# Mirrored score blocks through HBM in pieces of 512 bytes, with columns in runs of 32, and a new plan order

## The chip, the cores and the metric

The kernel runs on one core of a Trainium2 chip. The metric is the device time of one execution in microseconds (us); the time given is the median of several runs.

## The reference

Sixteen graphs (batches) of 1024 nodes with 128 features pass through four layers, all in float32, each with a residual: `x = x + layer(relu(layernorm(x)), adj)`. `adj` is a dense 1024 x 1024 matrix per batch, of which about 1.6% is non-zero.

```python
# layer 0, three times (i = 0, 1, 2; relu on all but the last)
h = h @ W[i] + b[i]
nh = h / norm(h)
h = (adj * (nh @ nh.T)) @ h
# layer 1
h = relu(((1 + eps) * h + adj.T @ h) @ W1 + b1) @ W2 + b2
# layer 2: attention, tanh(s1[i] + s2[j]) where adj > 0, softmax over j, times h
# layer 3: e = (h @ A) @ h.T; e = e + e.T; softmax(where(adj > 0, e, 0), axis=1) * adj, times h,
#          then three sigmoid gates per node
```

Two score matrices are symmetric: `nh @ nh.T` in layer 0 and `e + e.T` in layer 3. A batch that uses both has four such products of 1024 x 1024: three in layer 0 and one in layer 3.

## The kernel before

**Tiling.** Nodes are cut into 8 blocks of 128. A score matrix is made row block by row block (j = 0 to 7), each in two halves of four column blocks (`HALVES`, s = 0 and 1), and each half is one PSUM tile of 128 x 512 called `sq`. From it the VectorEngine (DVE) makes the weights: `ew = sq * rn * adjT` at line 1589 in layer 0, or the masked scores `e` with their maximum at line 1854 in layer 3. The TensorEngine (PE) then accumulates the weights with `h` into PSUM tiles `acc` (line 1422 by rows of 512, line 1433 by nodes of 128).

**The symmetric half.** `Square.row` computes only blocks on and above the diagonal (line 1360). A block below it is the transpose of one above. `Square.keep` saves those above from PSUM into the tile `above`, 22 blocks of 128 columns, at the places that `PLACE` gives. There are two ways back:

- Near the diagonal, the ScalarEngine (ACT) copies the blocks (line 1392), and PE transposes them when the lower row comes (line 1370).
- For the quarter of rows 4 to 7 by columns 0 to 3, in products where `by_dma` holds (batches 1 to 13, 13 x 4 = 52 products), DVE transposes every 32 x 32 square within the 128 x 512 tile (line 1382, four times in a product). After rows 1 and 3, `send` puts eight blocks into a buffer in HBM (`by_hbm`, line 1402, one DMA of 512 KB), and four DMAs of 128 KB bring the squares back to their mirrored places in the tile `got` (line 1413). `row` then hands out `got` in place of a PSUM tile for rows 4 to 7, s = 0.

In `by_hbm`, a row of 128 floats holds four squares that belong to four different partition groups of `got`, so a read moves pieces of 32 floats, 128 bytes.

**Other DMAs.** The transposed adjacency (`adjT`, line 1509) and some transposes of node features (`squares`, line 1186) use the same way of 32 x 32 squares, with pieces of 128 bytes. `adjL` (line 1467) and `x` (line 1450) come in longer pieces. All of them and the mirrored blocks are issued on the SyncEngine's queue (SP).

**Order.** The program is not written in its order of execution. Each operation is recorded with an engine, an estimated time, what it reads and writes, and a due time from the table `TIMES` (plus `PERIOD` per batch; the suffixes `<0`, `<1`, `>1`, `>0` are for the first two and last two batches, the key without a suffix for those between). `Plan.order` walks through estimated time: it takes the engine that can start earliest, and among that engine's operations ready within `WINDOW` (0.05 us) of it the one with the lowest rank:

```python
due = TIMES[o.key + o.edge if o.key + o.edge in TIMES else o.key][o.nth]
o.rank = (o.batch * PERIOD + due, o.seq)
```

`POOLS` and `KINDS` set how many buffers of a kind there are, how many may be held at once, and how many by batches younger than the oldest. So several batches run through one another, and every engine carries out its instructions in the order of the plan. The plan charges 0.35 x 2 us for a `by_hbm` write and 1.8 x 2 us for the four `got` reads, with latencies of 2.2 and 2.4 us.

**Names for the steps.** `psP` is the projection of `hT` with a weight (line 1200); `hT` is evicted from `acc` by ACT (line 1222); `hTn` is the transpose of `h`, the operand of the square; `rn` holds the inverse squared norms.

Of the kernel before, what the change touches and what calls it, by code (L numbers as in the profile page):

```python
# [12 lines left out]
ALU = mybir.AluOpType  # L13
AX = mybir.AxisListType

P = 128
# [205 lines left out]
def tile_adj_preln(  # L222
# [102 lines left out]
    for load_it in first:  # L325
# [13 lines left out]
        "adjT": ("adjT", 16, 16), "adjL": ("adjL", 5, 5), "x": ("x", 3, 3), "w4": ("big", 11, 5),  # L339
        "chunk": ("big", 13, 11), "above": ("above", 2, 2), "got": ("got", 1, 1), "ps": ("bank", 8, 7),  # L340
        "acc": ("bank", 8, 7), "small": ("small", 7, 18), "row": ("row", 5, 6), "hbm": ("hbm", 3, 3),
# [5 lines left out]
        "T DMA raw <0": [49.7, -29.05, 16.55, 2.15, 37.95, 6.2, 10.3, 13.25],  # L347
        "T PE raw <0": [7.8, -3.3, -0.1, -1.05, 0.65, 10.35, 23.15, 14.4, 9.05, 23.7, 22, 29.65, 26.65, 30.6,
            38.9, 41],
        "T ACT adjT <0": [2.9, 32.7, 7.85, 8.05, 13.45, 9.6, 13.2, 15.2, 18.4, 28.65, 29.8, 34.35, 33.9,  # L350
            38.45, 39.6, 39.65],
        "T DVE su <0": [54],
        "x DMA x <0": [49.15, -28],
        "0 DVE st <0": [5.7, 4.2],
        "0 DVE mv <0": [9.65],
        "0 POOL rstd <0": [2.6],
        "0 DVE nb <0": [9.1],
        "0 DVE hn <0": [9.1],
        "0 ACT hn <0": [30.5],
        "0 PE ps <0": [-0.85, -4.05],  # L360
        "0 ACT hT <0": [-21.45, 7.65],
        "00 PE psP <0": [6.6, -12.45],
        "00 DVE h <0": [14.75, 13.15],
        "00 PE ps <0": [21.35, 2.95],
        "00 ACT hTn <0": [11.15, 11.6],
        "00 ACT sq <0": [5.15, 12.1],
        "00 DVE ss <0": [2.95, 17.5, 18.2],
        "00 POOL rn <0": [30.3],
        "00 PE sq <0": [4.2, 22.45, 6.05, 6.9, 12, 7.4, 9.35, -26.35, 5.2, 26.95, 20.6, 21.8, 29.65, 25.9,
            26.55, 27.25, 31.3, 42.4, 46.3, 24.05, 51.65, 46.5],  # L370
        "00 ACT above <0": [12.45, 21.55, 15.8, 17.1, 16.7, 22.75, 22.65, 30.8, 38.15, 35.2],
        "00 DVE ew <0": [20.65, 22.5, 22.6, 36.95, 26.95, 33.7, 29.1, 35.05, 29.6, 44.15, 35.25, 41.45, 48.8,
            51.7, 45.3, 54.4],
        "00 PE acc0 <0": [0, 11.1, 10.4, 9.05, 15.65, 16.65, 19.7, 23.2, 28.65, 45.65, 34.25, 39.85, 31.35,
            54.3, 44.2, 64.05],
        "00 POOL params <0": [35.05, 40.7, 43.85, 51.55, 56.35, 57.25, 76.7],
        "00 DMA params <0": [52.85],
        "00 DVE params <0": [65.65, 68.1, 68.15, 77.5, 77.95],
        "00 PE params <0": [50.55, 59.35, 66.9],
        "00 ACT hT <0": [51.3, 54],  # L380
        "01 PE psP <0": [47.6, 63.65],
        "01 DVE h <0": [69.95, 78.75],
        "01 PE ps <0": [61.05, 52.95],
        "01 ACT hTn <0": [69.25, 72.45],
        "01 ACT sq <0": [69.7, 71.15],
        "01 DVE ss <0": [76.45, 78.15, 75.45],
        "01 POOL rn <0": [84.25],
        "01 PE sq <0": [68.25, 64.9, 66.25, 69.95, 68.2, 60.6, 70.8, 71.45, 81.95, 78.25, 78.75, 81.15,
            80.55, 85.85, 84.35, 87.05, 85.5, 86.8, 87.75, 84.5, 87.75, 79.1],
        "01 ACT above <0": [72.2, 74.55, 76.2, 75.5, 83.2, 81.35, 84.35, 84.75, 92.9, 94.75],  # L390
        "01 DVE ew <0": [78.15, 92.4, 81.55, 86.8, 87.85, 85.5, 93, 91.7, 93.05, 101.05, 89.5, 98.7, 96.5,
            111.15, 94.25, 91.55],
        "01 PE acc0 <0": [72.7, 84, 78.85, 78.6, 79.65, 78.25, 84.45, 78.05, 85.7, 85.9, 84.65, 87.6, 87.45,
            91.5, 89.15, 92.05],
        "01 ACT hT <0": [97, 99.95],
        "02 PE psP <0": [92.4, 92.15],
        "02 DVE h <0": [111.65, 105.7],
        "02 PE ps <0": [94.65, 94.55],
        "02 ACT hTn <0": [109.1, 104.6],
        "02 ACT sq <0": [106.2, 98.2],  # L400
        "02 DVE ss <0": [108.35, 109.3, 110.85],
        "02 POOL rn <0": [131.5],
        "02 PE sq <0": [103.1, 100.15, 107.65, 110, 101.65, 105.05, 100.95, 91.9, 107.7, 108.8, 108.7, 114,
            114.45, 111, 117.45, 118.85, 121.8, 110.4, 111.4, 123.9, 120.8, 128.25],
        "02 ACT above <0": [109.85, 113, 103.2, 116.3, 113.65, 115.55, 120.5, 124.45, 131.85, 139.8],
        "02 DVE ew <0": [113.25, 106.15, 118, 112.45, 125.7, 120.05, 121.65, 124.9, 130.25, 128.35, 126.65,
            132.8, 124.95, 126.9, 123, 141.6],
        "02 PE acc0 <0": [90.15, 114.45, 106.85, 103.9, 110.45, 112.95, 116.3, 111.45, 125.35, 117.1, 121.95,
            130.1, 112.45, 124.05, 123.15, 120.6],
        "02 DVE x <0": [136.55, 141.55],  # L410
        "T DMA adjT <1": [-129, -138.55, -158.15, -107.7, -154.45, -138.3, -107.8, -104.7],
        "T DVE adjT <1": [-118.3, -111.9, -110.5, -104.85, -101.8, -89, -85.8, -85.05],
        "T ACT adjT <1": [-117.75, -118.25, -112.75, -111.85, -103.3, -98.6, -96, -94.9],
        "1 DVE st <0": [135.95, 138.05],
        "1 DVE mv <0": [141.5],
        "1 POOL rstd <0": [134.7],
        "1 DVE nb <0": [144.5],
        "1 DVE hn <0": [140.8],
        "1 ACT hn <0": [134.3, 134.75],
        "1 DVE x <0": [146.55, 166.45, 168],  # L420
        "1 DMA adjL <0": [49.7, 59.55, 62.4, 63.35, 48, 159, 152, 151.35],
        "1 DVE adjL <0": [80.85, 77.2, 82.45, 79, 78.25, 151.75, 156.5, 161.35],
        "1 PE acc1 <0": [134.5, 135.3, 136.2, 137, 138.5, 133.15, 142.35, 139.75, 142.8, 141.1, 147.5,
            146.05, 148.15, 145.4, 151.95, 150.35],
        "1 ACT g <0": [157.9, 152.5],
        "1 PE py <0": [148.1, 149.8, 154.65, 147.75],
        "1 ACT y1 <0": [150.4, 163, 157.05, 152.1],
        "1 PE py2 <0": [152.35, 154.2],
        "2 DVE st <0": [171.4, 171.55],
        "2 DVE mv <0": [176.05],  # L430
        "2 POOL rstd <0": [176.55],
        "2 DVE nb <0": [173.9],
        "2 DVE hn <0": [173.85],
        "2 ACT hn <0": [184, 172.8],
        "2 PE ps <0": [162, 177.1],
        "2 ACT hnT <0": [180.45, 171.9],
        "2 DVE alone <0": [56.3],
        "2 DVE x <0": [183.6, 216.45, 216.65],
        "2 PE psP <0": [180.2, 166.35, 167.75],
        "2 ACT h <0": [176.5, 180.2, 180.6],  # L440
        "2 DVE hrow <0": [176.1],
        "2 PE pf <0": [171.3],
        "2 ACT hfl <0": [183.15],
        "2 PE pt <0": [174.35],
        "2 ACT sr <0": [180.15],
        "2 DMA sd <0": [283.8],
        "2 DMA s1 <0": [230.2],
        "2 DVE h <0": [175.5],
        "2 ACT e2 <0": [186.9, 189.9, 184.6, 189.95, 190.8, 191.25, 189.25, 193.65, 194, 192.5, 194.7, 197.1,
            198.05, 200.15, 199.1, 197.05],  # L450
        "2 DVE e2 <0": [195.1, 187.55, 193.65, 194.5, 199.55, 199.6, 196.4, 198.2, 201.75, 200.6, 203.8,
            206.9, 206.25, 208.1, 207.45, 208.75],
        "2 PE acc2 <0": [186.85, 186.2, 184.15, 189.1, 194.4, 197.45, 194.9, 188.8, 187.75, 198.65, 189.3,
            188.2, 194.8, 201.05, 196.95, 200.75, 197.1, 199.85, 195.55, 197.6, 198.5, 195, 197.75, 199],
        "2 DVE rden <0": [210.05, 211, 214.85, 213.35],
        "3 DVE st <0": [214.65, 213.1],
        "3 DVE mv <0": [246.2],
        "3 POOL rstd <0": [230.15],
        "3 DVE nb <0": [191.15],
        "3 DVE hn <0": [197.2],  # L460
        "3 ACT hn <0": [220.35, 225.45],
        "3 PE ps <0": [220.35, 209.3, 217.3, 213.95],
        "3 ACT hnT <0": [217.95, 221.55],
        "3 PE pg <0": [214.85, 222.65],
        "3 ACT gT <0": [221.05, 225.75],
        "3 PE psP <0": [228.55, 206.05, 224.15],
        "3 DVE h <0": [228.15, 223.85, 227.05],
        "3 ACT h3T <0": [219.7, 220],
        "3 ACT mask <0": [8.25, 18.4, 14.05, 26, 16.05, 23.05, 27.85, 30.25, 28.2, 40.5, 248.85, 250, 222.55,
            229.15, 237.05, 239.9],  # L470
# [679 lines left out]
    def by_block(t, w=D, n=NB):  # L1150
        return t[:, 0 : n * w].rearrange("p (c d) -> p c d", d=w)
# [976 lines left out]
```

## Time and profile before

| | us |
|---|---|
| median of 3 runs (2389.21 to 2389.68) | 2389.58 |
| the profiled execution | 2389.48 |
| its span, first to last instruction | 2387.7 |
| PE busy | 2349.2 |
| DVE busy | 2029.0 |
| ACT busy | 1435.5 |

The span is what the profile divides up; 1.8 us of the profiled execution lie around it. A busy time is the union of an engine's instructions. A matmul's end is modelled in the profile and overlaps the next one's start, so a PE that counts as busy may still have lost time between two starts. In rows of groups, "x" is a count, then come busy us and the mean ns of one, then the idle time just before and what ended it. The DMA share is the mean over the core's 16 DMA engines; it can exceed 1 where packets overlap.

### The profile page before, as it was taken

Reading aid. Unit: us, or ns where it says so; the run is one execution under the profiler, and the core shown is the slowest. Engines: PE = TensorE matmul, PEld = TensorE weight load, DVE = VectorE, ACT = ScalarE, POOL = GpSimd, SP = SyncE. Lnnn points to the kernel's source line nnn. Section 1 sums busy time; section 2 is a strip of 40 time slices with the busy share of each in tenths; the row PEclk is TensorE's granted clock in tenths of the full one; section 3 lists DMA queues with packets and bytes.
Section 4 is the critical chain, followed back from the end, with each engine's and each line's share of the span. In section 5 each row is a group of like instructions: output and inputs, shape, how many; then the busy total and the mean of one; then the engine's idle time right before and its main releaser. Section 6 shows DMA issues by size and latency. Waiting matters only on the chain.

```text
span 2387.7 us, 35098 instructions
## 1 busy us (share of the span) xinstructions
PE 2349.2 (98%) x11577; PEld 1548.5 (65%) x11577; DVE 2029.0 (85%) x5570; ACT 1435.5 (60%) x2561; POOL 246.8 (10%) x168
## 2 busy tenths in 40 slices
PE   8999999999999999999999999999999999999997
PEld 5568566675766657666575666757576575765764
DVE  6658798898988989899898988989899888987676
ACT  7325765756566465755756657465765656655475
POOL 3001010100101101010100101001011010110012
PEclk9999999999999999999999999999999999999999
DMA  9342949879596886959779497796968869165000
GB/s 197 85 107 63 172 91 180 153 128 178 115 177 141 139 171 130 171 123 166 157 129 181 108 181 146 137 164 130 171 139 149 164 129 169 45 107 124 1 27 18
DMA packets 1316743, 314.31 MB, mean 132 GB/s; under 512 B 1108441, under 2 KB 1298017, under 8 KB 1316561
## 3 DMA queue, kind: packets, MB, share of 16 engines
q1 hardware_dynamic: 1296400, 301.35, 67.6%
q10 hardware_dynamic: 19264, 9.70, 1.4%
q8 instruction: 92, 1.51, 0.3%
q0 software_dynamic: 896, 1.01, 0.2%
q14 instruction: 91, 0.74, 0.1%
HBM read 227.50 MB, written 84.47 MB: 131 GB/s over the span
## 4 chain that ended last, share of the span: by engine, by line
PE 85%; DMA 5%; SPq 4%; ACT 3%; DVE 3%; issue 1%; DVEq 0%; ACTq 0%
PE acc L1422 33%; PE sq L1360 18%; PE acc L1433 17%; PE psP L1200 6%; PE sq L1370 4%; DMA by_hbm<-above 2%; PE py L1210 2%; DMA got<-by_hbm 2%; PE py L1651 2%; SPq L1413 1%; SPq L1509 1%; PE ps_hTn L1169 1%; PE pg L1210 1%; DVE ew L1589 1%; DMA adjT<-in_adj_dram 1%
## 5 line engine op out<-in xcount | busy, mean ns | idle before, releaser
L1422 PE MATMUL acc<-ew,h 128*128 128x512 f32 x1024 | 486.4, 597 | 8.0 <-DVE ew L1589 8.0
L1589 DVE SCALAR_TENSOR_TENSOR ew<-sq,rn,adjT 128x512 f32<-128x512 f32 x612 | 436.4, 740 | 59.4 <-PE sq L1370 24.4
L1360 PE MATMUL sq<-hTn 128*128 128x512 f32 (+3 forms) x1152 | 439.4, 488 | 0.8 <-ACT hTn L1222 0.4
L1392 ACT COPY above<-sq 128x384 f32<-128x384 f32 (+3 forms) x432 | 167.6, 393 | 365.1 <-PE sq L1370 263.1
L1360 PEld LDWEIGHTS sq<-hTn 128*128 128x128 f32 x1152 | 196.3, 191 | 148.0 <-issue 99.8
L1422 PEld LDWEIGHTS acc<-ew,h 128*128 128x128 f32 x1024 | 180.2, 191 | 169.9 <-issue 132.4
L1433 PEld LDWEIGHTS acc<-h,ew 128*128 128x128 f32 x2048 | 245.4, 192 | 35.9 <-issue 21.7
L1433 PE MATMUL acc<-h,ew 128*128 128x128 f32 x2048 | 253.3, 275 | 3.2 <-DVE ew L1589 3.2
L1433 PEld LDWEIGHTS acc<-h,e 128*128 128x128 f32 x2048 | 235.0, 192 | 17.2 <-issue 12.8
L1422 PE MATMUL acc<-e,hs 128*128 128x512 f32 x512 | 241.1, 594 | 1.3 <-ACT hs L1904 0.8
L1433 PE MATMUL acc<-h,e 128*128 128x129 f32 x2048 | 236.6, 275 | 1.1 <-DVE e L1763 1.1
L1422 PE MATMUL acc<-adjL,hn 128*128 128x512 f32 x512 | 232.9, 592 | 0.0
L1162 POOL TENSOR_TENSOR rstd<-ve,mhalf 128x8 f32<-128x8 f32 x64 | 105.0, 1641 | 1166.5 <-DVE ve L1281 1166.5
L1370 PEld LDWEIGHTS sq<-ident,above 128*128 128x128 f32 x960 | 124.4, 141 | 100.2 <-issue 76.5
L1854 DVE CUSTOM_DVE_ANT_0 e<-mask,sq 128x512 f32<-128x512 int8 x204 | 137.4, 680 | 60.6 <-ACT above L1392 53.2
L1520 ACT ACTIVATE adjT<-adjT 128x1024 f32<-128x1024 f32 x120 | 126.6, 1055 | 97.8 <-DVE adjT L1517 90.4
L1895 DVE TENSOR_TENSOR e<-e,adjT 128x512 f32<-128x512 f32 x248 | 166.1, 680 | 18.2 <-ACT e L1886 18.1
L1382 DVE STREAM_TRANSPOSE above<-sq 128x512 f32<-128x512 f32 x208 | 145.7, 706 | 35.5 <-PE sq L1360 35.5
L1370 PE MATMUL sq<-ident,above 128*128 128x128 f32 x960 | 172.5, 273 | 1.5 <-ACT above L1392 1.5
L1763 DVE SCALAR_TENSOR_TENSOR e<-adjT,e 128x512 f32<-128x512 f32 x256 | 162.3, 689 | 5.5 <-ACT e L1759 5.3
L1422 PEld LDWEIGHTS acc<-adjL,hn 128*128 128x128 f32 x512 | 93.6, 190 | 102.3 <-issue 90.9
L1517 DVE STREAM_TRANSPOSE adjT<-adjT 128x1024 f32<-128x1024 f32 x120 | 148.6, 1239 | 8.8 <-DMA adjT<-in_adj_dram 8.4
(164 smaller groups left out, 3587.2 us busy)
## 6 DMA issues: line engine op xcount, KB each, us to landing
adjL<-in_adj_dram SPq DMA_DIRECT2D x128, 512.0 KB
adjT<-in_adj_dram SPq DMA_DIRECT2D x480, 128.0 KB
by_hbm<-above SPq DMA_DIRECT2D x104, 512.0 KB
got<-by_hbm SPq DMA_DIRECT2D x416, 128.0 KB
s<-sd SPq DMA_DIRECT2D x15, 512.0 KB
out_dram<-z ACTq DMA_DIRECT2D x15, 512.0 KB
d_hT<-hn SPq DMA_DIRECT2D x14, 512.0 KB
hT<-d_hT SPq DMA_DIRECT2D x56, 128.0 KB
```

Source lines behind the costliest of these rows:

```text
L1200: nc.tensor.matmul(dst.t[:, (c - lo) * n : (c - lo + 1) * n], cols(srcT.t, c), w, start=True, stop=True)
L1360: lambda: nc.tensor.matmul(dst.t[:, (first - lo) * P :], cols(leftT.t, j), span(rightT.t, first, hi), start=True, stop=True),
L1370: nc.tensor.transpose(cols(dst.t, r), cols(above.t, p), ident)
L1382: lambda: nc.vector.transpose(span(above.t, p, p + 4), read.t),
L1392: lambda: nc.scalar.copy(span(above.t, p, p + hi - first), read.t[:, (first - lo) * P :]),
L1422: lambda s=s, lo=lo, hi=hi: nc.tensor.matmul(acc[s].t, cols(h.t, at, w), span(ew.t, lo, hi), start=(j == 0), stop=(j == NB - 1)),
L1433: nc.tensor.matmul(a.t[:, (c - lo) * n : (c - lo + 1) * n], cols(ew.t, c), h.t[:, at * w : at * w + n], start=(j == 0 and c == lo), stop=( ...
L1517: dve(V(N), [t], [t], lambda t=t: nc.vector.transpose(t.t, t.t), True)
L1589: lambda view=view, ew=ew, rn=rn, j=j, lo=lo, hi=hi: nc.vector.scalar_tensor_tensor(by_block(span(ew.t, lo, hi), D, 4), view(), rn.t[:, j ...
L1763: lambda e=e, j=j, lo=lo, hi=hi: nc.vector.scalar_tensor_tensor(span(e.t, lo, hi), span(aT[j].t, lo, hi), 0.0, span(e.t, lo, hi), op0=ALU. ...
L1854: lambda e=e, view=view, mask=mask, peak=peak, s=s, lo=lo, hi=hi: nc.vector.tensor_tensor_reduce(by_block(span(e.t, lo, hi), D, 4), by_blo ...
L1895: lambda e=e, j=j, lo=lo, hi=hi: nc.vector.tensor_mul(span(e.t, lo, hi), span(e.t, lo, hi), span(aT[j].t, lo, hi)),
```

## The change

Three things change.

1. `keep`: DVE's transpose of a 32 x 32 square stays, but it reads its PSUM tile and writes `above` in another order. The eight blocks of a pair of rows are laid out as (h, r, q, i): h is the place of a square within its 128 columns (four of them), r the row of the pair, q the column block (four), i the 32 columns of a square. One block of 128 floats now holds four squares that go to the same partition group of `got`.
2. `send` and `row`: the write to HBM keeps its pieces of 512 bytes. Each of the four reads takes 256 whole rows of 128 floats, in pieces of 512 bytes, into 32 partitions of `got`. In `got`, the 512 columns of a row q are then no longer four runs of 128 but 16 runs of 32, each 128 floats from the next, and the DVE operations that read it (lines 1589 and 1854) get views of 16 x 32 for all their operands; with a PSUM tile their views stay 4 x 128.
3. `TIMES`: nearly all due times are replaced, and the limits in `KINDS` for `w4`, `chunk`, `above`, `ps`, `acc`, `small` and `row` change. `POOLS`, `PERIOD`, `AHEAD`, `WINDOW` and the costs that the plan charges for the DMAs are the same.

```diff
-        "adjT": ("adjT", 16, 16), "adjL": ("adjL", 5, 5), "x": ("x", 3, 3), "w4": ("big", 11, 5),
-        "chunk": ("big", 13, 11), "above": ("above", 2, 2), "got": ("got", 1, 1), "ps": ("bank", 8, 7),
-        "acc": ("bank", 8, 7), "small": ("small", 7, 18), "row": ("row", 5, 6), "hbm": ("hbm", 3, 3),
+        "adjT": ("adjT", 16, 16), "adjL": ("adjL", 5, 5), "x": ("x", 3, 3), "w4": ("big", 9, 5),
+        "chunk": ("big", 10, 12), "above": ("above", 2, 1), "got": ("got", 1, 1), "ps": ("bank", 7, 8),
+        "acc": ("bank", 7, 8), "small": ("small", 7, 16), "row": ("row", 3, 3), "hbm": ("hbm", 3, 3),
...
-        "00 DVE ew <1": [-96, -97.05, -94.35, -97.1, -95.9, -87.65, -86.4, -88, -83.3, -75.3, -82.2, -75.35,
+        "00 DVE ew <1": [-97.85, -102.05, -94.45, -97.2, -96, -87.75, -86.5, -88.1, -93.95, -75.4, -82.3, -74.75,
...
-        "00 PE acc0 <1": [-98.65, -96.15, -97.8, -100.25, -96.3, -85.8, -86.2, -91.2, -92.3, -98.5, -80.2,
+        "00 PE acc0 <1": [-97.5, -95, -96.65, -85.6, -83.9, -76.4, -85, -84, -103.3, -86.3, -79.05, -75.15,
...
-        "01 ACT hT": [59.4, -161.95],
-        "02 PE psP": [11.7, 50.15],
+        "01 ACT hT": [71.05, 59.7],
+        "02 PE psP": [46.1, 46.55],
...
+    def like(v, t):
+        return t.rearrange("p (x i) -> p x i", i=v.shape[2])
...
-                return self.got, lambda: self.got.t.rearrange("p (r c d) -> p c r d", r=QUARTER, d=P)[:, q]
+                return self.got, lambda: self.got.t.rearrange("p (x q i) -> p q x i", q=QUARTER, i=SQ)[:, q]
...
-                    lambda: nc.vector.transpose(span(above.t, p, p + 4), read.t),
+                    lambda: nc.vector.transpose(
+                        self.apart(j // 2).rearrange("p (h r q i) -> p r h q i", r=2, q=QUARTER, i=SQ)[:, j % 2],
+                        read.t.rearrange("p (q h i) -> p h q i", h=P // SQ, i=SQ),
+                    ),
...
+        def apart(self, pair):
+            return span(self.above.t, 6 + 8 * pair, 14 + 8 * pair)
...
             def squares_to_places():
-                src = by_hbm.t.rearrange("(x j) (g i) -> g j x i", j=SQ, i=SQ)
-                for g in range(P // SQ):
-                    dst = span(got.t, lo * 4, hi * 4)[g * SQ : (g + 1) * SQ]
-                    with nc.allow_non_contiguous_dma(reason="squares"):
-                        nc.sync.dma_start(dst.rearrange("p (x i) -> p x i", i=SQ), src[g])
+                src = by_hbm.t.rearrange("(h y j) f -> h j y f", h=P // SQ, j=SQ)
+                dst = by_block(span(got.t, lo * 4, hi * 4))
+                for h in range(P // SQ):
+                    nc.sync.dma_start(dst[h * SQ : (h + 1) * SQ], src[h])
...
-                            by_block(span(ew.t, lo, hi), D, 4), view(), rn.t[:, j : j + 1],
-                            by_block(span(aT[j].t, lo, hi), D, 4), op0=ALU.mult, op1=ALU.mult,
+                            like(view(), span(ew.t, lo, hi)), view(), rn.t[:, j : j + 1],
+                            like(view(), span(aT[j].t, lo, hi)), op0=ALU.mult, op1=ALU.mult,
```

The `TIMES` entries shown are those that the prediction speaks of; the reads of `e` from `got` at line 1854 change as those of `ew` do.

## The prediction

> **What bounds the kernel now.** I read the engine totals first, then the chain, then PE's own waits, and only then the DMA side.
>
> ```profile
> PE 2349.2 (98%) x11577; PEld 1548.5 (65%) x11577; DVE 2029.0 (85%) x5570; ACT 1435.5 (60%) x2561; POOL 246.8 (10%) x168
> ...
> PE 85%; DMA 5%; SPq 4%; ACT 3%; DVE 3%; issue 1%; DVEq 0%; ACTq 0%
> ```
>
> PE is busy 98% of the span and is 85% of the chain that ended last. Because ends of matmuls are modelled, I also took the start-to-start times of the matmuls in the trace, by width. The lower quartile is 429 ns for 512 columns and 109 to 111 ns for 128 to 131. At those pitches all 11,577 matmuls take 2311.8 us. The rest of the 2387.7 us span is 7.3 us before the first matmul, 10.8 us after the start of the last, and 57.8 us of lost time between; 44.4 us of that sits in 186 gaps over 30 ns, and 12.9 us of those 44.4 in the first 100 us. The change adds and removes no PE instruction, so **the 44 us are all that it can win or multiply**. The waits of PE and DVE say whose they are:
>
> ```profile
> PE acc L1422 <- DVE ew L1589: 8.0, 8, 4.3
> ...
> PE psP L1200 <- ACT hT L1222: 3.2, 13, 0.3
> ```
>
> ```profile
> DVE ew L1589 <- DMA got<-by_hbm: 22.7, 18, 8.2
> ```
>
> Columns: total us, times, longest us. The largest wait of PE is for `ew`, and more than half of it is one wait of 4.3 us. DVE in turn has one wait of 8.2 us for `got`, the tile that the change touches. The timeline puts both in one place, in batch 1's first product:
>
> ```profile
> 58.20 7.13 SPq L1413 DMA_DIRECT2D got<-by_hbm  x8
> ...
> 69.48 2.74 DVE L1589 SCALAR_TENSOR_TENSOR ew<-got,rn,adjT 128x512 f32<-128x512 f32 x4 [8.23 <-DMA got<-by_hbm]
> 70.28 2.07 PE L1422 MATMUL acc<-ew,h 128*128 128x512 f32 x2 [4.25 <-DVE ew L1589]
> ```
>
> ```profile
> 60.00:66.00 6.00, 6.00 (x15) 2.42 (x13) 0.89 (x2) 2.12 (x4) 0.00 (x0) 1.00 1.33 179
> 66.00:72.00 6.00, 1.75 (x3) 0.83 (x3) 2.52 (x4) 0.37 (x1) 0.00 (x0) 0.78 1.14 300
> 72.00:78.00 6.00, 6.00 (x13) 3.04 (x12) 2.42 (x5) 0.66 (x2) 0.00 (x0) 0.65 0.20 81
> ```
>
> In the windows the last three numbers are PE clock, DMA share and GB/s. The DMA engines are overfull (1.33, 1.14) while the eight `got` reads go through; PE then waits, and comes back at a clock of 0.65.
>
> [...] the 4.25 us wait is followed by a clock of 0.65. [...] on q1 the packet records average 15.6 ns for 128 B and 28.6 ns for 512 B, so four times the bytes take 1.83 times as long. [...] No row of this trace has runs of 32 words with hops.
>
> **The change, part by part.**
>
> (1) Reads of `got`. 416 DMAs of 128 KB stay 416, but each goes from 1024 pieces of 128 B to 256 of 512 B. Before: 416 x 1024 x 15.6 ns / 16 engines = 415 us of DMA time in the span. After: 416 x 256 x 28.6 / 16 = 190 us. So q1's 67.6% should fall by 225 / 2388 = 9.4 points, to some 58%. For one read of four DMAs: 4.0 us becomes 1.8 us. At 58.20 us there are eight: 8.0 becomes 3.7, which is 4.3 us earlier. `ew` would start near 65.2 instead of 69.48, and end at 65.9. PE ran out of other work at 66.03 (the last transpose starts at 65.70 and takes 0.33), so **the wait of 4.25 us goes**. With it goes the slow clock: 0.35 x 6 us in 72 to 78, and half of the 1.7 us run after 70.28, together 3.0 us. Sum 7.3 us.
>
> In the middle I find three more `got` waits that PE feels, at 1168, 1312 and 1889 us: DVE waits 0.93, 1.24 and 1.36, all shorter than the 2.2 us that a read saves, and PE waits 0.2, 0.5 and 0.6, sum 1.3 us. What is late next there is the product itself: at 815 and 1104 us the same instruction waits 1.75 us for PE's `sq`, and no DMA helps that. The other `got` waits are under PE work and are worth nothing. The writes `by_hbm` keep 1024 pieces of 512 B: nothing.
>
> (2) The same transposes with pieces, and reads in runs of 32. The rows now:
>
> ```profile
> L1382 DVE STREAM_TRANSPOSE above<-sq 128x512 f32<-128x512 f32 x208 | 145.7, 706 | 35.5 <-PE sq L1360 35.5
> ...
> L1589 DVE SCALAR_TENSOR_TENSOR ew<-got,rn,adjT 128x512 f32<-128x512 f32 x156 | 112.0, 748 | 37.2 <-DMA got<-by_hbm 22.7 <-PE sq L1360 5.9 <-PE acc L1433 5.5
> ```
>
> The second line is matched by 740 ns for the form from PSUM, so where the operand lies hardly matters. I take 706 and 748 for after as well[...]. Below: the shortest transpose seen is 673 ns, 33 x 208 = 7 us of DVE time, all under PE. [...] The cover is DVE's idle time, 359 us in all, but only 6 to 14 us per 100 us in the middle[...]. I take nothing.
>
> (3) Order and limits. Nearly every due time moves, and so do the limits on buffers held at once (`w4` 11 to 9, `row` 5,6 to 3,3, and so on). No instruction is added. In the first two batches the PE numbers mostly rise by 1.1, those of ACT by 5.35 and those of DVE fall by 0.1; since an engine's instructions are ranked against one another only, that keeps most of the start's order. In the interior it doesn't: the 126 ACT numbers move by 8 on average, with a spread of 24. The trace of before can't price this. Below: the 13 waits for `hT` cost PE 0.41 us each as a gap (5.4 us), an early gap at 39.6 us costs 1.5, and half the 7.7 us of gaps in the last 88 us could go: 11 us. Above: the third rival. I take zero.
>
> Sum against the profiled execution (2389.48 us, 1.8 us of it outside the span, 0.1 under the median): 2389.5 - 7.3 - 1.3 = 2380.9. The median stands so close that I forecast **2381 us**.
>
> **Rivals.**
> *The wait stays in another form.* The new numbers rank batch 1's first `ew` from `got` some 10.6 earlier (-83.3 to -93.95) and its accumulation 11 earlier (-92.3 to -103.3), and the same DMA queue gets adjacency loads in another order. DVE is served in order, so if this instruction stands further forward, the 4.3 us that the read gains are given back: other `ew` behind it wait[...]. Then only the 1.3 us of the middle is won: 2388. For it: the two full windows hold 1.33 x 6 + 1.14 x 6 = 14.8 us of DMA work, and `got` is at most 8.0 of it. Against it: the plan still charges a read 3.6 us, so it does not place the consumer earlier than the data by its own reckoning.
>
> *Slower: the eviction of `hT` loses its place.* In the interior, the second half of `hT` after the second product (L1222) was due at -161.95, ahead of everything that ACT had ready; now it is due at 59.7, behind whatever is ready with a lower number. Behind it PE has only four transposes and then the projection `psP`, in order. ACT is 60% busy, and its common instructions take 1.05 us (`adjT`, `mask`) to 1.14 us (`e`). One of these in front in each of 13 batches costs 13 x 1.14 = 14.8 us if PE has nothing else placed there: 2381 + 15 = 2396. It decides from 8.6 / 13 = 0.66 us lost per batch, one such instruction in 8 of 13 batches. For it: PE already waits there 13 times. Against it: the projection's own numbers move too (11.7 and 50.15 to 46.1 and 46.55), so other PE work may be put in front.
>
> **How the numbers follow.** The forecast gets 0.60; its own range is 2369 (with the 11 us) to 2385. The wait that stays gets 0.16, at 2385 to 2393. The slower case gets 0.24, of which 0.04 is for transposes or reads that double; 2394 to 2405. A measurement of this kernel can tell 0.2% (4.8 us) from no change. So: faster 0.60, same 0.16, slower 0.24. The range 2366 to 2398 leaves out about a tenth at each end.
>
> **What would show it.** Right: q1 falls to about 58% and its packets by 416 x 768 = 319,488 to some 977,000; no wait for `got` above 4 us near 70 us, and no clock under 0.9 in that stretch; `above` transposes near 706 ns and `ew` from `got` near 748. Wrong in (1): packets fall and the clock still dips there. Wrong in (2): a transpose above 1.0 us, and DVE above 90% busy. Wrong in (3): more than 5 us of new PE waits for `hT`, `ew` or `e` in the middle. PE busy should fall by a few us, its instructions stay 11,577.

## The result, and the profile after

| | before | after |
|---|---|---|
| median us (range, runs) | 2389.58 (2387.41 to 2391.98, 7) | 2381.50 (2379.62 to 2384.38, 7) |
| profiled execution, its span | 2389.48, 2387.7 | 2384.38, 2382.6 |

The ratio is 0.9964, 95% interval 0.9953 to 0.9976: the changed kernel is faster by 8 us. The profiled execution of after is the longest of its seven, which matters for the start below; a second profile of the same kernel, `a0_changed_again`, is of 2381.0 us, the shortest of its twelve. The two stand for a slow and a quick start.

The engine totals, the chain's shares and the queue of the page of after:

```profile
PE 2346.0 (98%) x11577; PEld 1552.4 (65%) x11577; DVE 2038.7 (86%) x5570; ACT 1435.5 (60%) x2561; POOL 247.7 (10%) x168
...
PE 95%; ACT 2%; DVE 1%; SPq 1%; DMA 1%; issue 0%; POOL 0%; DVEq 0%; ACTq 0%; POOLq 0%
...
q1 hardware_dynamic: 976912, 301.35, 61.0%
```

In the chain, DMA and SP's queue had 9% before and have 2% now. The count of packets is the predicted one. The DVE groups, one row per form:

```profile
L1385 DVE STREAM_TRANSPOSE above<-sq 128x512 f32<-128x512 f32 x208 | 146.0, 703 | 28.7 <-PE sq L1363 28.5
...
L1598 DVE SCALAR_TENSOR_TENSOR ew<-got,rn,adjT 128x512 f32<-128x512 f32 x156 | 111.7, 745 | 12.9 <-DMA adjL<-in_adj_dram 6.8 <-DMA got<-by_hbm 1.5 <-PE ps_hnT L1172 1.1
```

The new access pattern costs DVE nothing (transposes 703 ns after 706, reads of `got` 745 after 748). What changed is the idle time ahead of the `ew` that reads `got`: 12.9 us after 37.2. The waits of PE (total us, times, longest us):

```profile
PE acc L1431 <- DVE ew L1598: 4.3, 2, 4.0
PE acc L1431 <- ACT hs L1913: 4.3, 2, 3.3
PE psP L1203 <- ACT hT L1225: 3.0, 12, 0.3
PE acc L1442 <- DVE e L1772: 1.9, 2, 1.6
PE pf L1713 <- DVE hrow L1706: 1.1, 1, 1.1
```

Of the eight waits for `ew` that reached 4.3 us at the longest, two are left, but the long one is still there. New is a wait of 3.3 us for `hs`, the scaled `h` of layer 3. So I divided what PE loses by place. As in the prediction, lost time is the sum of start-to-start times of matmuls above their dense pitch; the dense part is 2311.8 us in every kernel with 11,577 matmuls.

| PE's lost us | 0 to 100 | 100 to 2100 | from 2100 |
|---|---|---|---|
| before | 13.2 | 34.3 | 10.2 |
| after | 11.3 | 26.0 | 14.8 |
| `a0_changed_again` | 8.4 | 25.9 | 14.8 |
| `e1_layout_only` | 7.2 | 26.4 | 10.0 |
| `e1b_layout_again` | 10.5 | 26.8 | 10.0 |
| `e2_order_only` | 13.4 | 29.6 | 15.0 |

**The gain lies in the middle (8.3 us), part of it is given back at the end (4.6 us), and the start varies from one execution to the next.** The first sum, -1.9 - 8.3 + 4.6 = -5.6, stands beside spans that differ by 5.1; for `a0_changed_again` it is -8.6 beside 8.5.

**The start.** The timeline of after (start, length, engine, line, tile; in brackets the idle time before and its releaser):

```profile
55.86 0.96 SPq L1412 DMA_DIRECT2D by_hbm<-above  x1
58.26 6.41 SPq L1422 DMA_DIRECT2D got<-by_hbm  x8
68.22 2.74 DVE L1598 SCALAR_TENSOR_TENSOR ew<-got,rn,adjT 128x512 f32<-128x512 f32 x4 [6.85 <-DMA adjL<-in_adj_dram]
69.02 2.07 PE L1431 MATMUL acc<-ew,h 128*128 128x512 f32 x2 [4.02 <-DVE ew L1598]
```

and its windows (busy us and counts of PE, PEld, DVE, ACT and POOL, then clock, DMA share, GB/s):

```profile
60.00:66.00 6.00, 5.00 (x13) 2.04 (x11) 0.17 (x1) 2.60 (x5) 0.00 (x0) 1.00 0.95 227
66.00:72.00 6.00, 2.98 (x6) 1.66 (x7) 3.40 (x5) 0.00 (x0) 0.00 (x0) 0.64 0.98 333
```

The eight reads are one line of the timeline, but not one block: they belong to two pairs of rows. The trace's DMA records show the second pair's write landing at 62.82 and its first read going out at 62.89, so SP stands still from 60.57 to then. (Before, that write had landed at 61.35, while SP was still issuing the first pair's reads, until 61.72.) The eight issues take 6.41 us (7.13 before), and from the first issue to the last landing the reads take 9.6 us (58.26 to 67.90) after 11.0 (58.20 to 69.16). The releaser `adjL` in the row of `ew` is no operand of it; `ew` starts 0.32 us after the last read has landed, in both kernels. It starts 1.26 us earlier than before, and PE arrives there 1.0 us earlier too, at 65.0. The wait is 4.02 us after 4.25, and the slow clock stays (0.64 after 0.78 in 66 to 72 us, 0.79 after 0.65 in 72 to 78).

**The middle.** Timelines of before, then of after, at one of the two waits that the prediction gave to PE's `sq`:

```profile
804.70 5.86 SPq L1413 DMA_DIRECT2D got<-by_hbm  x8
...
814.34 0.75 DVE L1589 SCALAR_TENSOR_TENSOR ew<-got,rn,adjT 128x512 f32<-128x512 f32 x1 [1.75 <-PE sq L1360]
```

```profile
800.01 4.22 SPq L1422 DMA_DIRECT2D got<-by_hbm  x7
...
808.56 0.75 DVE L1598 SCALAR_TENSOR_TENSOR ew<-got,rn,adjT 128x512 f32<-128x512 f32 x1
```

The second view starts at 800 us, so it shows seven of the eight reads; the first went out at 799.64. `ew` from `got` does not read `sq`; the releaser is a name inferred from the last event, and the instruction stood for `got`, whose last read landed at 813.92. In `e1_layout_only` below, where every engine keeps its order of before, the same `ew` starts at 804.73, ahead of that `sq` at 805.32. PE lost 1.19 us there and 1.21 us at 1104, and loses neither now.

**The transfer.** From the DMA records of all 104 groups of four reads (medians, us):

| | write landing | four reads, issue to landing | write's issue to reads landed |
|---|---|---|---|
| before | 3.95 | 6.51 | 11.19 |
| after | 3.60 | 5.17 | 9.50 |
| `e1_layout_only` | 3.57 | 5.17 | 9.41 |
| `e2_order_only` | 3.77 | 6.58 | 11.22 |

### The profile page after: what moved, and what is told of

Same layout as the page of the kernel before. It is cut to its first block, busy times and chain, and to the rows that moved or that the text cites. A ratio compares the mean times of both kernels' runs of the same rounds, so it can differ in the third digit from the quotient of the medians.

```text
span 2382.6 us, 35138 instructions
## 1 busy us (share of the span) xinstructions
PE 2346.0 (98%) x11577; PEld 1552.4 (65%) x11577; DVE 2038.7 (86%) x5570; ACT 1435.5 (60%) x2561; POOL 247.7 (10%) x168
## 4 chain that ended last, share of the span: by engine, by line
PE 95%; ACT 2%; DVE 1%; SPq 1%; DMA 1%; issue 0%; POOL 0%; DVEq 0%; ACTq 0%; POOLq 0%
PE acc L1431 36%; PE sq L1363 20%; PE acc L1442 19%; PE psP L1203 6%; PE sq L1373 4%; PE py L1660 2%; PE py L1213 2%; PE psN L1203 1%; PE pg L1213 1%; PE ps_hTn L1172 1%; SPq L1518 1%; PE ps_hnT L1172 1%; PE ps_h3T L1172 1%; DMA raw<-in_adj_dram 0%; ACT hT L1225 0%
## 5 line engine op out<-in xcount | busy, mean ns | idle before, releaser
L1431 PEld LDWEIGHTS acc<-e,hs 128*128 128x128 f32 x512 | 92.4, 190 | 98.5 <-issue 75.0
```

The lines of the kernel that those rows point to most:

```text
L1431: lambda s=s, lo=lo, hi=hi: nc.tensor.matmul(acc[s].t, cols(h.t, at, w), span(ew.t, lo, hi), start=(j == 0), stop=(j == NB - 1)),
```

## The experiments

Where an expectation uses a letter, it stands for a theory; the question is put in words ahead of each. "Layout" is the new order of squares with 512-byte reads, "order" is `TIMES` with the limits in `KINDS`.

### Layout and order apart

`e1_layout_only` is the code of after with the limits and due times of before; every engine's order of instructions is that of before. `e1b_layout_again` is the same kernel on another chip, `a0_changed_again` is after on that chip, to see how far the start varies. `e2_order_only` is the code of before with the limits and due times of after.

```diff
 # e1, e1b: the code of after
-    KINDS, TIMES of after
+    KINDS, TIMES of before
 # e2: the code of before
-    KINDS, TIMES of before
+    KINDS, TIMES of after
```

> The layout and the 512-byte reads of the change, with the due times and limits of the kernel before: every engine's instruction order is that of before. Theory A (the gain comes from reads that land earlier): most of the 8 us appears here, 2381 to 2385 us; the waits of ew for got at 815, 1104, 1168, 1312, 1889 and 1970 us are gone (some 5 us of PE gaps), while the wait near 70 us stays at about 4 us, because the second pair's write lands late there in any case. Theory B (the gain comes from the new order): 2388 to 2390 us and those gaps stay. Both expect transposes near 705 ns and ew from got near 745 ns.

> The due times and limits of the change, with the old layout and reads in pieces of 128 bytes: every engine's instruction order is that of the changed kernel. Theory A: near or above the kernel before, 2387 to 2393 us, with ew waiting for got in the middle batches again. Theory B: 2380 to 2384 us, with few waits for got.

> The layout and reads of the change with the order of before, a second time: 2375 to 2379 us. Its gaps after 2100 us stay near 10 us. The wait near 70 us was 2.1 us in the first profile, with no slow clock[...].

> The changed kernel once more, next to the layout alone on one chip. If the new order costs what the first profiles say (4 us at the start, 5 us at the end), it is 4 to 6 us slower than the layout alone: 2380 to 2383 us against 2376 to 2378. In its profile the gaps at the end are again near 15 us after 2100 us, since they belong to the order; the wait near 70 us may be shorter or longer, since the adjacency loads ahead of it went at 1.09 to 1.26 us each in the profiles so far.

| | median (range) | before beside it | ratio (interval) |
|---|---|---|---|
| e1 | 2376.57 (2375.52 to 2379.77) | 2389.54 | 0.9952 (0.9940 to 0.9965) |
| e1b | 2379.28 (2378.12 to 2379.76) | 2388.84 | 0.9958 (0.9945 to 0.9970) |
| a0 | 2383.75 (2381.00 to 2385.27) | 2388.84 | 0.9978 (0.9969 to 0.9986) |
| e2 | 2390.38 (2387.72 to 2394.35) | 2389.54 | 1.0004 (0.9996 to 1.0012) |

The layout alone is worth 9.6 to 13.0 us, more than the whole change and more than either theory had put on e1; the order alone is worth nothing. The order on top of the layout costs 0.9978 against 0.9958 on one chip, 4.5 us. The table of lost time shows why the two don't add up. With the old layout the new order saves 4.7 us in the middle (34.3 to 29.6) and loses 4.8 at the end; with the new layout the middle has nothing more to save (26.4 to 26.0), and the end still loses 4.8. Both parts cure the same middle waits: there DVE's idle time ahead of `ew` from `got` is 29.0 us before, 22.2 in e2, 8.0 in e1 and 6.0 in after. Only the order brings the end's. PE's waits in e2 show the old start and the new end together:

```profile
PE acc L1421 <- DVE ew L1588: 7.2, 3, 6.3
PE acc L1421 <- ACT hs L1903: 4.3, 2, 3.3
```

In e1 no wait for `hs` is above 0.9 us:

```profile
PE acc L1432 <- DVE ew L1599: 2.9, 3, 2.1
...
PE acc L1432 <- ACT hs L1914: 0.9, 1, 0.9
```

DVE's busy time is 2029.6 us in e1 (2029.0 before) and 2037.4 in e2, so the 10 us more of DVE in after come with the order, not with the views of 16 x 32.

In e1 and before, each matmul can be set beside itself, since the order is the same. Between 100 and 2100 us the products that take `ew` have all of e1's gain; the two waits at 815 and 1104 us are 2.4 us of it, and the rest is spread over many smaller ones.

### How much of a read is small pieces

Ahead of every four reads of `got`, `e5_dose_of_pieces` issues two more reads of 128 KB each in pieces of 128 bytes, into a tile that nobody reads; `e8_half_dose` issues one. Both have the layout of after and the order of before.

```diff
+                more = by_hbm.t.rearrange("(y p) (g i) -> g p y i", p=P, i=SQ)
+                for g in range(2):          # e8: range(1)
+                        nc.sync.dma_start(
+                            spare[:, g * 2 * P : (g + 1) * 2 * P].rearrange("p (y i) -> p y i", i=SQ), more[g]
+                        )
                 for h in range(P // SQ):
                     nc.sync.dma_start(dst[h * SQ : (h + 1) * SQ], src[h])
```

> The layout alone with the order of before, and ahead of each four got reads two more reads of 128 KB from the same buffer in pieces of 128 bytes into a tile that nobody uses: 2048 pieces x 15.6 ns / 16 = 2.0 us more DMA time per read and two more issues on SP, about the 2.2 us that the change saves. Nothing else differs. Theory A (time of the reads): 2386 to 2391 us, with the got waits near 815, 1104, 1168, 1312, 1889 back. Rival (the gain lies in the way the blocks lie in HBM or in got, or in DVE): stays under 2380 us. At the start the extra reads of the second pair must also wait for those of the first, so the wait there may exceed that of before.

> The layout alone with one extra read of 128 KB in pieces of 128 bytes ahead of each four got reads, half of the former dose, 1.0 us of DMA time by the packet records. From the issue of a write to the landing of its reads the medians so far are 9.4 us for the layout alone (2376.6 to 2379.3 us), 11.2 for the kernel before (2389) and 12.7 for the full dose (2441). Theory A (only this landing time counts): between 10.4 and 11.3 us here and a time of 2380 to 2390 us. Rival (the extra reads hurt for another reason, such as SP being held): the landing stays under 10.4 us and the time is above 2390, or the time does not move.

e5: 2441.30 (2436.52 to 2442.70), ratio 1.0215 (1.0201 to 1.0229). e8: 2396.98 (2395.25 to 2402.38), ratio 1.0045 (1.0033 to 1.0058). The direction was right; the times that theory A gave, 2386 to 2391 and 2380 to 2390 us, were far too low. DVE's waits for `got` in e5, and in e8:

```profile
DVE ew L1606 <- DMA got<-by_hbm: 84.8, 36, 10.4
```

```profile
DVE ew L1606 <- DMA got<-by_hbm: 39.3, 26, 8.0
```

Five kernels share nearly one order of instructions (`e7` is told below). From 100 to 2100 us, the idle time of DVE ahead of `ew` from `got` ranks PE's lost time and the medians, but for the first two rows, which lie close together and overlap in their intervals:

| | idle ahead of `ew` from `got`, us, 100 to 2100 | PE's lost us, 100 to 2100 | median us |
|---|---|---|---|
| e7 | 7.1 | 27.5 | 2375.69 |
| e1, e1b | 8.0, 8.8 | 26.4, 26.8 | 2376.57, 2379.28 |
| before | 29.0 | 34.3 | 2387.89 to 2389.58 |
| e8 | 37.8 | 42.3 | 2396.98 |
| e5 | 87.6 | 80.6 | 2441.30 |

The way from late reads to time is shown, and it is steep: from before to e5 59 us of idle DVE cost 46 us of PE. The median landing does not tell it. In e8 the median from the write's issue to the reads' landing is 11.21 us, that of before is 11.19, and e8 is still 9 us slower. The added DMA is also issued on SP (the write's issue to the first `got` read takes 5.46 us, 4.65 before). Counted from the end of the last DVE transpose that a product's second write needs, its reads land 0.15 us later in e8 than in before, on average of the 52 products. The write goes out 0.12 us later and lands 0.07 later still; the first read goes out 0.69 us later after that, and the reads themselves are 0.74 quicker. DVE then waits 0.17 us longer, 52 times, 8.6 us in all. So e8's loss also goes with late reads of `got`, and what makes them late is the added read in front of them and the time for which it holds SP. How much each of these two does is not shown.

### What holds the start

`e4_reads_first` asks whether the `adjL` load of 512 KB that SP issues between the first two writes delays the reads: it is put behind the second pair's reads in batch 1, with the other `adjL` loads of batch 0. The rival is that the transport of the whole start sets it, and that another order of the same transfers brings nothing.

```diff
+    behind = [o for o in plan.ops if o.key == "00 DMA got" and o.batch == 1][1]
+    for o in plan.ops:
+        if o.key == "1 DMA adjL" and o.batch == 0:
+            plan.place_after(o, behind)
```

> The changed kernel, with the first adjacency load of layer 1 of batch 0 (512 KB) issued behind the eight got reads of batch 1's first product, not ahead of the second write by_hbm. PE's instruction order is unchanged. Theory C (the wait near 70 us is for the second pair's write, which lands at 62.8 us behind that load, and only then are its reads issued): the second pair's reads are issued near 59 to 60 us, the PE wait falls from 4.0 to under 2 us, the clock does not drop, and the time falls by 4 to 6 us against the changed kernel. Rival D (the DMA engines are full up to then whatever the order of the queue): reads end less than 1 us earlier, the wait stays at 3 to 4 us, and the time stays within 2 us.

It ran in 2382.47 (2381.61 to 2384.45), ratio 0.9973 (0.9963 to 0.9983), within 1 us of after. Its timeline:

```profile
61.57 3.80 SPq L1422 DMA_DIRECT2D got<-by_hbm  x8
...
70.13 2.08 PE L1431 MATMUL acc<-ew,h 128*128 128x512 f32 x2 [5.09 <-DVE ew L1598]
```

Now the eight reads are one block of 3.80 us, but it starts at 61.57, 3.3 us later than in after. That delay is a side effect of the edit, as SP's waits between 50 and 60 us show:

```profile
SPq L1518 <- DMA x<-in_x_dram: 4.3, 1, 4.3
```

```profile
50.36 0.37 ACTq L1459 DMA_DIRECT2D x<-in_x_dram  x1
```

Once the `adjL` load was held back, the plan moved a load of `x`, 512 KB as well, from 76.98 us to 50.36. (Three of the loads of `x`, this one among them, go out on ACT's queue and not on SP's.) It signals its landing on the same semaphore as the next-to-last `adjT` load, so SP stood from 52.39 to 56.74 until `x` had landed at 56.72. After has no such wait. From the first write's issue to the last read's landing e4 took 11.3 us, against 13.0 to 15.2 in after, a0, e1 and e1b, but the same 4.3 us of standing still came first, and PE waited 5.09 us. So e4 changed two things at the start and decides between neither theory: it shows only that both together move the time by less than 2 us. Whether the `adjL` load alone delays the reads stays open.

`e6_start_by_pe` takes the DMA out of the question: batch 1's first product sends no blocks through HBM, and PE transposes them, 16 transposes more. It is after with that; `e7_layout_start_by_pe` is e1 with that.

```diff
-            square = Square(k, hTn, hTn, "abc"[i] in FLAGS and far(b, i))
+            square = Square(k, hTn, hTn, "abc"[i] in FLAGS and far(b, i) and not (b == 1 and i == 0))
 # and due times for the four PE and four ACT steps that this adds to "00 PE sq <1" and "00 ACT above <1"
```

> The changed kernel with the first product of batch 1 alone not sent through HBM: ACT copies its quarter and PE transposes it, 16 transposes at 0.11 us = 1.8 us more PE work. Theory F (what the changed kernel still loses near 70 us is the wait for got and the slow clock after it, 4.2 + 2.6 us): 4 to 6 us faster than the changed kernel, and no clock below 0.9 there. Rival G (the adjacency tiles come too late there anyway, so the wait moves to them): within 2 us of the changed kernel.

> The layout and reads of the change in the order of before, and the first product of batch 1 not sent through HBM (16 more PE transposes, 1.8 us). In the two profiles of the layout alone the start lost 7.2 and 10.5 us, in that of the same edit on the changed kernel 5.6. If the wait near 70 us is what varies, this is 0 to 3 us faster than the layout alone (2376.6 and 2379.3 us in two jobs), 2375 to 2378, and the fastest of all; if not, it is slower than the layout alone by the 1.8 us of transposes.

e6: 2379.76 (2378.83 to 2381.21), ratio 0.9961 (0.9948 to 0.9973), 4.0 us under a0 on the same chip. e7: **2375.69 (2374.48 to 2376.57), ratio 0.9949 (0.9936 to 0.9963)**, the lowest median of all. Its interval lies below that of a0; it overlaps those of e1 and of after's first comparison. The windows of e6, then of e7:

```profile
66.00:72.00 6.00, 6.00 (x22) 3.25 (x21) 2.77 (x8) 1.68 (x4) 0.00 (x0) 1.00 0.00 0
```

```profile
66.00:72.00 6.00, 6.00 (x28) 3.65 (x27) 5.17 (x20) 1.83 (x4) 0.00 (x0) 1.00 0.00 0
```

PE doesn't stop there, the clock is 1.00, and the DMA share is 0.00. Lost time in the first 100 us falls from 8.4 (a0) to 5.6 in e6, and from 7.2 or 10.5 to 3.7 in e7; against it stand the 16 transposes, 1.7 us.

### What holds the end

`e3_old_tail` is after with the due times of before for the last batch, to see whether these entries alone make the new waits.

```diff
-    TIMES["... >0"] of after
+    TIMES["... >0"] of before
```

> The changed kernel with the due times of the last batch alone taken from the kernel before. In the profiles, PE lost 10.4 us in gaps over 30 ns after 2300 us in the changed kernel against 7.7 before, one of 3.4 us in front of acc<-e,hs. Theory E (the last batch's new order gives some of the gain back): 2 to 5 us faster than the changed kernel, 2377 to 2380 us. Rival: the gaps move but their sum stays, within 2 us of 2381.

It missed: 2399.47 (2398.71 to 2400.15), ratio 1.0046 (1.0032 to 1.0059). PE's lost time from 2100 us on is 29.9 us, twice that of after. Its waits of PE from 2100 us on:

```profile
PE acc L1442 <- DVE e L1772: 5.1, 2, 4.8
PE acc L1431 <- ACT hs L1913: 4.0, 2, 3.1
PE acc L1431 <- DVE e L1904: 3.3, 1, 3.3
```

So the due times of this batch could not be exchanged alone. A likely reason, not tested, is that they rank its operations against the neighbour's, which kept the new ones. e1 and e2 show that the end's loss comes with the order, and the traces show the waits, but which entry makes them is not settled. The place itself is plain in the timeline of `a0_changed_again`:

```profile
2343.83 1.05 ACT L1976 ACTIVATE z<-z 128x1024 f32<-128x1024 f32 x1
2344.91 1.15 ACT L1977 ACTIVATE z<-z,half 128x1024 f32<-128x1024 f32 x1
2345.96 0.38 ACT L1913 ACTIVATE hs<-h,sum 128x128 f32<-128x128 f32 x1
2346.40 1.81 PE L1431 MATMUL acc<-e,hs 128*128 128x512 f32 x2 [3.25 <-ACT hs L1913]
```

ACT runs two gates' `z`, 1.05 and 1.15 us, ahead of an `hs` of 0.38 us, and PE has nothing ordered in front of the product that needs it. In after this wait of 3.3 us is followed by half clock for 3.41 us, from 2351.21 to 2354.62 (a clock of 0.54 in the window below). In e4 the same wait is not (1.00), and PE loses 13.2 us from 2100 us on where after loses 14.8; so of the 4.6 us some 1.6 are the slow clock. The windows of after, then of e4:

```profile
2351.00:2354.00 3.00, 3.00 (x12) 1.86 (x11) 2.06 (x7) 0.68 (x3) 2.92 (x2) 0.54 0.03 5
```

```profile
2351.00:2354.00 3.00, 3.00 (x17) 1.97 (x16) 2.67 (x11) 1.54 (x5) 2.92 (x2) 1.00 0.03 5
```

## Why the prediction was right in its sum and wrong in its terms

2381.0 was forecast and 2381.5 measured. **That closeness is partly luck: three terms were off, and they cancel.** The working that says so, lost time of PE against before:

| term | predicted | after | a0 |
|---|---|---|---|
| (1) start | -7.3 | -1.9 | -4.8 |
| (1) middle | -1.3 | -8.3 | -8.4 |
| (3) order, at the end | 0 | +4.6 | +4.6 |
| sum | -8.6 | -5.6 | -8.6 |

- **Step (1), what a read saves: mis-sized.** The forecast for four reads was 2.2 us of 4.0; from issue to landing the median fell from 6.51 to 5.17, by 1.34 us. Most of the difference is the price of a packet. The 28.6 ns were the mean of q1's 170,616 packets of 512 bytes before, and none of these is a read of `got`. The packets of 128 bytes took 403 us less in all, near the 415 of the forecast, but those of 512 bytes took 249 us more, not 190. That is a net 1.5 us for each of the 104 groups of four, and it is why q1 is at 61.0% and not 58. If the other packets kept their time, the new ones took 37.4 ns each. With no other packets under way (15 groups before, 16 after) a packet of `got` took 14.2 ns before and 31.5 after. The forecast had the direction right: alone, the packets of four reads took 3.6 us of the 16 engines before and 2.0 after.
- **Step (1), "the wait of 4.25 us goes": failed in after's profile.** The step put eight reads into one block that shrinks by 4.3 us. They are two groups with a write's landing between them, and from first issue to last landing they shrank by 1.3 us. What was named as wrong ("packets fall and the clock still dips there") is what after shows. It is what the rival "the wait stays in another form" named. The reason that this rival gave, the new order, is not seen to matter: PE waits 2.08 and 3.02 us with the old order (e1, e1b), 4.02 and 2.25 us with the new one (after, a0). Whether adjacency loads in front of the reads share in it e4 leaves open. e6 and e7 show what the place is worth without the DMA.
- **Step (1), the middle: mis-sized by a misreading.** "No DMA helps that" was said of the waits at 815 and 1104 us because the row named PE's `sq`. The instruction has no such operand. And three waits were counted where the loss is spread over many: e1, with before's order throughout, loses 7.9 us less in the middle, and the doses of e5 and e8 drive the same loss the other way.
- **Step (2): right.** Transposes 703 ns, reads 745 ns, and `e` from `got` 670 after 680. That the times of before would stay was the author's estimate. The rows of after bear it out: runs of 32 words with hops took 745 ns where runs of 128 took 748.
- **Step (3), order at zero: mis-sized.** Its upper bound was hung on the third rival, the slower case by waits for `hT`, and these are 3.0 us in 12 after 3.2 in 13. The cost came in another place, at `hs`, `e` and `hrow` of the last batches, which the prediction priced only as a possible gain ("half the 7.7 us of gaps in the last 88 us could go").

So the forecast "faster" was right for its main reason, reads in larger pieces that free `ew` earlier, though the place was the middle and not the start.

## What to carry to other kernels

Price a transfer through HBM by the whole chain (write issued, write landed, reads issued, reads landed), not by the packets: here four times fewer packets took 15% off that chain. Take a packet's price from packets that go the same way (alone, one of 512 bytes took 26.7 ns in the writes and 31.5 in the reads), and expect the new size to have a price of its own (14.2 ns at 128 bytes in the reads). When a layout and an order are changed together, measure each alone; an order that hides a wait is worth nothing once the wait is gone, and keeps its own price. Before a wait is called out of reach, see whether the named releaser is an operand of the waiting instruction. After moving one transfer, see what else the plan has moved with it.

## What the runs showed of the hardware

**Pieces and issue.** A packet of the `by_hbm` writes took 26.7 ns with no other DMA under way (4 writes in after), against 31.5 ns for one of the same 512 bytes in the reads. SP is also held less by DMAs of fewer pieces here. The rows of the tile `got` (minimum, median and longest ns of an issue), before and then after:

```profile
L1413 SPq DMA_DIRECT2D got<-by_hbm x416: 302/650/3469, 58.2 to 2135.1; - x139
```

```profile
L1422 SPq DMA_DIRECT2D got<-by_hbm x416: 302/448/1800, 58.3 to 2123.6; - x139
```

The mean fell from 757 to 467 ns, 416 x 0.29 = 121 us of SP over the span. Nothing in the prediction priced that.

**Half clock after a wait of 2.25 us.** The wait that the prediction set beside a slow clock was one of 4.25 us. Here one of 2.25 us was followed by the slow clock as well. The windows of `a0_changed_again`, then of `e1_layout_only`, whose wait was 2.08 us:

```profile
66.00:69.00 3.00, 2.34 (x4) 1.21 (x5) 3.00 (x5) 0.00 (x0) 0.00 (x0) 0.60 1.02 410
69.00:72.00 3.00, 3.00 (x9) 1.67 (x8) 1.80 (x4) 0.27 (x1) 0.00 (x0) 0.83 0.27 105
```

```profile
66.00:69.00 3.00, 1.55 (x6) 0.97 (x7) 2.36 (x4) 0.00 (x0) 0.00 (x0) 1.00 1.03 412
69.00:72.00 3.00, 3.00 (x10) 1.40 (x8) 2.50 (x5) 0.42 (x2) 0.00 (x0) 1.00 0.44 175
```

a0 has a clock of 0.60 and 0.83 there, e1 one of 1.00 in both windows. Length alone does not decide it: the wait of 3.3 us for `hs` near the end of e4 kept full clock (1.00 in 2351 to 2354).

The clock records of before and after say more. In these two traces the granted clock is 1.0 or 0.5, and it changes only at whole multiples of 3.41 us from the start of the first record. Cut into these stretches, the two traces hold five at full clock that were followed by half clock. PE (by its modelled ends) was idle for 3.39 and 3.08 us of those in before, and for 2.69, 1.99 and 3.18 us of those in after. In the 1,376 stretches after which full clock went on, it was idle for at most 1.55 us. The wait of 3.26 us for `hs` in after put 1.26 us into one stretch, which full clock followed, and 1.99 us into the next, which half clock followed. Whether e4's wait was divided differently is not shown. Between matmuls, half clock lasted 6.83 us in before, and 6.83 and 3.41 us in after.

The length of the half clock is part of why one kernel's start loses 8.4 us in one execution and 11.3 in another: it was 6.83 us in after, and in a0 3.4 us by the two windows above ((0.40 + 0.17) x 3 / 0.5).
